# Turning the score maxima of a cross-attention round by transfers through device memory instead of on TensorE

## The chip, the cores and the metric

The kernel runs on one core of a Trainium2 chip. The metric is the device time of one execution in microseconds (us), lower is better; runs of the kernel before gave 2155.49, 2155.64 and 2157.81 us, median 2155.64.

## The reference, cut to what matters

The model is two Perceiver layers over 32 batches of 64 latent rows of width 256. Most of the time goes to the cross-attention of the second layer, in which each batch's 64 latents attend, with 16 heads of 16 channels, to a context of 1601 rows:

```
q = query @ Wq.T + bq;  k = bank @ Wk.T + bk;  v = bank @ Wv.T + bv      # bank: (32, 1601, 256)
scores = einsum('bhqd,bhkd->bhqk', q / sqrt(16), k)
attn = softmax(scores, axis=-1)
ctx = einsum('bhqk,bhkd->bhqd', attn, v)
out = ctx @ Wo.T + bo
```

The softmax needs the maximum of each score row over the 1601 keys, and it is this maximum that the change is about. All other parts (self-attention, routed and shared experts, a recurrent block, a quantised feed-forward) are untouched; they run in the gaps of the loop described next.

## The kernel before

Two batches make one tile of 128 latent rows, so there are 16 *positions*. A position is worked in 13 *units* (`NU`): four *halves* (two batches times two groups of eight heads), each cut into three pieces of 512 keys, and one tail unit for the last 65 keys of all four halves. The main loop runs over the 208 units `g`, and in each iteration it does, in this order:

1. `column_scores(g)`: the scores of unit g with the keys on the partitions. Four bfloat16 matmuls (L770; L767 in the tail unit) first put the negative maxima into PSUM: a 3-row operand `neg`, three bfloat16 parts whose sum is the fp32 value, against ones. Then 16 matmuls (L776) add q·k on top, and ScalarE takes exp of the sum (L782), which gives `pt`.
2. `values(g + 4)`: V of a later unit (L230 `vps`), copied out by VectorE into `vau` (L712).
3. `maxima_rows(h)`, in the iterations where a half has been scanned to its end one iteration earlier: TensorE transposes `mxp` (L751) into a PSUM tile `tpm` of the ring `ps_mm`, and VectorE copies it out as `neg` (L753).
4. `run(g, 0)`: a piece of the other layers' work, laid out by a plan.
5. `row_scores(g + 5)`: the same scores with the latents on the partitions, for the maxima alone: eight matmul passes (L728 `r`) into two PSUM tiles of `ps_sc`, and one VectorE maximum over each (L735, L732 for the tail).
6. `maxima(h)`, when unit g + 5 is the last of a half: VectorE reduces to `ng` (128 x 4, negated, L741) and splits it into three bfloat16 parts in `mxp` (L743 to L746).
7. `weighted(g)`: 64 matmul passes of `pt` against `vau` (L800).
8. `keys(g + 6)`: K of a later unit (L230 `kps`), then `run(g, 1)`.

So a half's maxima are reduced at the end of step 6 of one iteration, turned round in step 3 of the next, and first read by step 1 of the one after that. There are 64 halves; the first is treated before the loop.

The order on TensorE, VectorE, ScalarE and GpSimd is the order of the program text; only the queue of SyncE (SP), which issues the loads and stores, is ordered by a scheduler. The halves' PSUM tiles: `r` and `s` share `ps_sc` (two tiles); `vps`, `kps`, `tpm` and the other layers' tiles share the ring `ps_mm` of three, so a tile waits until the tile three before it has been read out.

Of the kernel before, what the change touches and what calls it, by code (L numbers as in the profile page):

```python
# [9 lines left out]
F32 = mybir.dt.float32  # L10
BF16 = mybir.dt.bfloat16
AF = mybir.ActivationFunctionType
ALU = mybir.AluOpType
AX = mybir.AxisListType

P = 128
# [5 lines left out]
NT = NB * S // P  # L22
# [6 lines left out]
NP = L // PIECE  # L29
TAIL = L - NP * PIECE  # L30
NU = 4 * NP + 1
# [13 lines left out]
def perceiver_kernel(ctx: ExitStack, tc: tile.TileContext, a: dict, out: bass.AP):  # L45
    nc = tc.nc
    PSUM = bass.MemoryType.PSUM

    const = ctx.enter_context(tc.tile_pool(name="const", bufs=1))
    work = ctx.enter_context(tc.tile_pool(name="work", bufs=2))  # L50
# [7 lines left out]
    away = loop.enter_context(tc.tile_pool(name="away", bufs=2, space=bass.MemoryType.DRAM))  # L58
# [5 lines left out]
    def sc_tile(name):  # L64
        return ps_sc.tile([P, 2, 512], F32, tag="sc", name=name)
# [4 lines left out]
    def mm_tile(shape, name, dtype=F32):  # L70
        return ps_mm.tile(shape, dtype, tag="mm", name=name)
# [5 lines left out]
    def work_tile(shape, tag, name, dtype=F32):  # L77
        return work.tile(shape, dtype, tag=tag, name=name, bufs=BUFS.get(tag, 1))
# [25 lines left out]
    def load_rest(ti):  # L104

        t = big.tile([P, 2, 2, TAIL], F32, tag="rest", name=f"rest_{ti}", bufs=2)
        for b in range(2):
# [11 lines left out]
    identb = const.tile([P, P], BF16, name="identb")  # L119
# [3 lines left out]
    ones = const.tile([P, P], F32, name="ones")  # L123
# [5 lines left out]
                            base=0, pattern=[[-16, 8]], channel_multiplier=1)  # L129
    nc.gpsimd.affine_select(out=mask8, in_=mask8, compare_op=ALU.is_ge, fill=0.0,  # L130
                            base=15, pattern=[[16, 8]], channel_multiplier=-1)
# [31 lines left out]


    vau = [const.tile([P, 4, VW], F32, name=f"vau{k}") for k in range(5)]
    mxp = [const.tile([P, 4, 32], BF16, name=f"mxp{k}") for k in range(2)]
    for t in vau:
        nc.gpsimd.memset(t, 0.0)
        nc.gpsimd.memset(t[:, :, 0:VW - 16].rearrange("p k (h d) -> p k h d", d=17)[:, :, :, 16:17], 1.0)
    for t in mxp:  # L170
        nc.vector.memset(t, 0.0)


# [85 lines left out]
    def layer0(ti, csum, k=0, soon=False):  # L259
# [151 lines left out]
        for o, w in ((u_ps, w_s1), (v_ps, w_s3)):  # L411
            for oc in range(2):
# [22 lines left out]
                            pattern=[[1, E], [-1, E]], channel_multiplier=0)  # L435
# [211 lines left out]
    def scanned(g):  # L647

        pos, p = divmod(g, NU)
        return (pos, 4 * pos + (p - 1) // NP, (p - 1) % NP) if p else (pos, None, None)  # L650
# [65 lines left out]
    def row_scores(g):  # L716


        pos, h, k = scanned(g)
        w, qbd = wholes[pos], queries[pos]  # L720
        if h is None:
            w.mx = small.tile([P, 4, 4, NP + 1], F32, tag="mx1", name=f"mx1_{w.ti}", bufs=2)
        ps = [sc_tile(f"r_{g}_{m}") for m in range(2)]
        for q in range(4) if h is None else [h % 4]:
            for i in range(4):
                r = slice(32 * i, 32 * i + 32)
                o = ps[i // 2][:, i % 2, :] if h is not None else ps[i // 2][:, i % 2, q * TAIL:(q + 1) * TAIL]
                nc.tensor.matmul(o, lhsT=qbd[r, q % 2, q // 2].rearrange("p h q -> p (h q)"),  # L728
                                 rhs=w.kt[r, q, :] if h is None else halves[h].kt[k][r, :], start=True, stop=True)
        for m in range(2):  # L730
            if h is None:
                nc.vector.tensor_reduce(w.mx[:, 2 * m:2 * m + 2, :, NP],  # L732
                                        ps[m][:, :, :4 * TAIL].rearrange("p i (q l) -> p i q l", q=4), AX.X, ALU.max)
            else:
                nc.vector.tensor_reduce(w.mx[:, 2 * m:2 * m + 2, h % 4, k], ps[m], AX.X, ALU.max)  # L735

    def maxima(h):

        hf = halves[h]
        ng = small.tile([P, 4], F32, tag="ng", name=f"ng_{hf.name}")  # L740
        nc.vector.tensor_reduce(ng, wholes[hf.pos].mx[:, :, h % 4, :], AX.X, ALU.max, negate=True)  # L741
        m = mxp[h % 2]
        nc.vector.tensor_copy(m[:, :, 0], ng)  # L743
        nc.vector.tensor_tensor(ng, ng, m[:, :, 0], ALU.subtract)
        nc.vector.tensor_copy(m[:, :, 1], ng)
        nc.vector.tensor_tensor(m[:, :, 2], ng, m[:, :, 1], ALU.subtract)  # L746

    def maxima_rows(h):
        hf = halves[h]
        t = mm_tile([P, P], f"tpm_{hf.name}", BF16)  # L750
        nc.tensor.transpose(t, mxp[h % 2].rearrange("p i c -> p (i c)"), identb)  # L751
        hf.neg = work.tile([P, P], BF16, tag="neg", name=f"neg_{hf.name}", bufs=5)
        nc.vector.tensor_copy(hf.neg, t)  # L753

    def column_scores(g):
# [399 lines left out]
    def first_layer(pos, k=0):  # L1155
        x3[pos] = yield from layer0(order[pos], csums[pos], k)
# [10 lines left out]
    def first():  # L1167

        csum = sums_tile(order[0])
        steps = layer0(order[0], csum, 0, True)  # L1170
        next(steps)
        yield
        next(steps)
        yield
        next(steps)
        junk = big.tile([P, L], F32, tag="part", name="junk", bufs=1)
        for b in range(2):
            yield
            summed(order[0], csum, b, 0, ctxs[b][:, 0, :], junk)
            nc.vector.tensor_reduce(csum[:, 1, b:b + 1], ctxs[b][:, 1, :], AX.X, ALU.add)  # L1180
        csums[0] = csum
        yield
        x3[0] = yield from steps
        yield from query(0, x3[0])
# [7 lines left out]
    def early_sums():  # L1192
        for pos in range(1, 4):
            yield from sums(pos, 2)
# [3 lines left out]
    def planned(gen, t0, t1, n, place):  # L1198
        plan.append(Steps(gen, t0 * NU / 16, t1 * NU / 16, n, place))
# [20 lines left out]
    with tc.manual_schedule(engines={ET.PE, ET.DVE, ET.Activation, ET.Pool}):  # L1220
        ahead, beside, summing = Steps(first()), Steps(first_layer(1, 1)), Steps(early_sums())
        early = [lambda g=g: keys(g) for g in range(1, 4)] + [lambda: keys(0)] + [
            lambda g=g: values(g) for g in range(4)] + [lambda g=g: keys(g) for g in range(4, 6)]

        def others():
            if 0 in csums:
                summing.step()
            if 1 in csums:
                beside.step()

        ahead.step()
        late = [late_weights]
        while 0 not in queries:
            if early:
                early.pop(0)()
            ahead.step()
            others()
            if 1 in csums and late:
                late.pop()()
        for f in early + late:  # L1240
            f()
        for g in range(4):
            row_scores(g)
            others()
        maxima(0)
        row_scores(4)
        others()
        maxima_rows(0)
        if beside.gen is not None:
            plan.insert(0, Steps(beside.gen, 0, 3, 30 - beside.done, 2))  # L1250
        planned(biased(), 3, 5, 2, 1)
        if summing.gen is not None:
            plan.insert(0, Steps(summing.gen, 0, 5, 12, 0))
        planned(all_ternary(), 5, 23, 24, 2)

        def run(t, place):
            for s in [s for s in plan if s.t0 <= t]:
                s.run(t, place)
                if t >= s.t1 and t < NU * NT - 1:
                    s.all()  # L1260
                if s.gen is None:
                    plan.remove(s)

        for g in range(NU * NT):
            pos, p = divmod(g, NU)
            if pos + 1 < NT:
                if p == 0:
                    wholes[pos + 1].rest = load_rest(order[pos + 1])
                if p in (2, 9):
                    load_batch(2 * pos + 2 + p // 8)  # L1270
            column_scores(g)
            if g + 4 < NU * NT:
                values(g + 4)
            if p == 1 and pos:
                normalise(pos - 1)
            if g + 4 < NU * NT and scanned(g + 4)[2] == NP - 1:
                maxima_rows(scanned(g + 4)[1])
            run(g, 0)
            if g + 5 < NU * NT:
                row_scores(g + 5)  # L1280
                if scanned(g + 5)[2] == NP - 1:
                    maxima(scanned(g + 5)[1])
            weighted(g)
            if p == NU - 1:
                gathered(pos)
            if g + 6 < NU * NT:
                keys(g + 6)
            if p == 1 and pos:
                x4[pos - 1] = projected(pos - 1)
            run(g, 1)  # L1290
        normalise(NT - 1)
        x4[NT - 1] = projected(NT - 1)
        plan.append(Steps(second_layer(NT - 1)))
        while plan:
            for s in list(plan):
                s.step()
                if s.gen is None:
                    plan.remove(s)
# [46 lines left out]
```

## Time and profile before

| | |
|---|---|
| median of the runs | 2155.64 us |
| the profiled execution | 2154.58 us, of which span 2152.9 us |
| `r` matmuls (L728) | 1536 passes, mean 650 ns |
| row maxima (L735) | 384 of 1219 ns |
| transposes (L751) | 64, median 219 ns; their weight load 100 ns |
| copies of `neg` (L753) | 64 of 213 ns |
| `maxima` (L741, L743 to L746) | 64 each of 169, 176, 190, 177 and 177 ns |
| SP queue | 293 rows in the program; moves 129.52 MB, 17.6% of the 16 engines' time |

The granted TensorE clock is 1.00 over nearly all of the loop (0.974 as a mean over the span). The span has 95% of busy TensorE; the loop itself runs from about 94 us to 2080 us. "Busy" of TensorE is modelled and its matmuls overlap, so the distance between starts says more than the durations.

### The profile page before, as it was taken

The numbers are of one execution on the slowest core, as the hardware profiler recorded it, in microseconds if no ns is written. First come the engines' busy times: TensorE is split into PE (matmuls) and PEld (weight loads), VectorE is DVE, ScalarE is ACT, GpSimd is POOL, SyncE is SP. The second block draws the span as 40 slices with busy tenths as digits, with TensorE's granted clock in tenths as the row PEclk, the third lists the DMA queues.
The fourth block names the chain that finished last, engine by engine and source line by source line (L and its number), as shares of the span: only waits on it lengthen the run. The fifth ranks groups of instructions, "written<-read, shape, count | busy, mean of one in ns | idle before, by whom it ended". The sixth has DMA issues, their size and how long they took to land.

```text
span 2152.9 us, 69473 instructions
## 1 busy us (share of the span) xinstructions
PE 2034.8 (95%) x31691; PEld 1482.9 (69%) x31707; DVE 1302.2 (60%) x2614; ACT 907.1 (42%) x1400; POOL 324.7 (15%) x538
## 2 busy tenths in 40 slices
PE   5799999999999999999999999999999999999964
PEld 4567677777776777777777777767776666676753
DVE  4556756666656665665666656565676656565544
ACT  3334454444535444444444435453433334334332
POOL 2211211111112111112111111111100111000011
PEclk8799999999999999999999999999999999999986
DMA  7233212221212222112221212211111111101000
GB/s 267 84 107 115 95 66 75 68 75 35 74 67 71 73 68 67 45 66 75 68 75 40 91 33 79 75 38 42 45 45 32 47 42 35 54 2 45 2 14 5
DMA packets 52654, 134.77 MB, mean 63 GB/s; under 512 B 12894, under 2 KB 32776, under 8 KB 52360
## 3 DMA queue, kind: packets, MB, share of 16 engines
q1 hardware_dynamic: 51800, 129.52, 17.6%
q8 instruction: 248, 4.06, 0.8%
q10 hardware_dynamic: 560, 0.81, 0.1%
q14 instruction: 46, 0.38, 0.1%
HBM read 124.02 MB, written 6.29 MB: 61 GB/s over the span
## 4 chain that ended last, share of the span: by engine, by line
PE 84%; DVE 9%; ACT 3%; DMA 2%; issue 1%; POOL 1%; SPq 0%; POOLq 0%; DVEq 0%; ACTq 0%
PE vps L230 17%; PE kps L230 16%; PE r L728 10%; PE o L800 9%; PE s L776 8%; PE ff L230 4%; DVE mx L735 3%; PE s L770 3%; PE ffo L951 2%; PE q L230 1%; ACT pt L782 1%; PE wo L230 1%; PE hg L902 1%; PE s L330 1%; PE v L316 1%
## 5 line engine op out<-in xcount | busy, mean ns | idle before, releaser
L735 DVE TENSOR_REDUCE mx<-r 128x2 f32<-128x1024 f32 x384 | 451.9, 1219 | 131.2 <-PE r L728 131.1
L782 ACT ACTIVATE pt<-s 128x1024 f32<-128x1024 f32 (+1 forms) x416 | 403.0, 1020 | 286.0 <-PE s L776 285.8
L695 ACT ACTIVATE kt<-kps,chv 128x512 f32<-128x512 f32 x192 | 131.9, 687 | 636.1 <-PE kps L230 636.1
L230 PE MATMUL kps<-ctxT,w_L_xattn_WkT 128*128 128x512 f32 x768 | 384.5, 624 | 11.9 <-DMA ctxT<-ctxT 11.9
L230 PE MATMUL vps<-w_L_xattn_WvT,ctxT 128*128 128x128 f32 x3072 | 394.5, 282 | 0.0
L230 PEld LDWEIGHTS vps<-w_L_xattn_WvT,ctxT 128*128 128x128 f32 x3072 | 358.5, 192 | 23.7 <-issue 2.8
L712 DVE COPY vau<-vps 128x512 f32<-128x512 f32 (+1 forms) x208 | 143.4, 689 | 370.4 <-PE vps L230 370.4
L800 PEld LDWEIGHTS o<-pt,vau 128*32 128x32 f32 (+1 forms) x13312 | 196.7, 110 | 151.5 <-issue 139.7
L800 PE MATMUL o<-pt,vau 128*32 128x64 f32 (+1 forms) x13312 | 231.2, 221 | 5.3 <-ACT pt L782 5.2
L728 PE MATMUL r<-kt,qbd 32*128 32x512 f32 x1536 | 230.3, 650 | 1.9 <-DVE mx L735 1.1
L230 PEld LDWEIGHTS kps<-ctxT,w_L_xattn_WkT 128*128 128x128 f32 x768 | 132.0, 191 | 124.4 <-issue 107.5
L776 PEld LDWEIGHTS s<-qbd,kt 32*128 32x128 f32 x6144 | 206.2, 187 | 3.1
L776 PE MATMUL s<-qbd,kt 32*128 32x128 f32 x6144 | 207.3, 271 | 0.0
L242 ACT ACTIVATE part<-part 128x1601 f32<-128x1601 f32 x60 | 92.6, 1543 | 16.9 <-DMA part<-ctxT 16.6
L728 PEld LDWEIGHTS r<-kt,qbd 32*128 32x128 f32 x1536 | 65.7, 185 | 40.8 <-issue 18.5
L770 PE MATMUL s<-neg,onesb 3*128 3x512 bf16 x768 | 80.4, 385 | 6.7 <-DVE mx L735 4.5
L770 PEld LDWEIGHTS <-onesb 3*128 3x128 bf16 x768 | 20.9, 91 | 94.2 <-issue 92.5
L230 PE MATMUL ff<-nT,w_fg 128*128 128x128 f32 x384 | 51.7, 287 | 1.0 <-ACT nT L938 1.0
L308 POOL TENSOR_TENSOR kbd<-kT,mask 128x512 f32<-128x512 f32 x32 | 32.7, 1043 | 129.9 <-ACT kT L301 129.9
L230 PEld LDWEIGHTS ff<-nT,w_fg 128*128 128x128 f32 x384 | 47.8, 200 | 1.9 <-ACT nT L938 1.8
L230 PE MATMUL ff<-nT,w_fv 128*128 128x128 f32 x384 | 48.9, 278 | 0.0
L230 PEld LDWEIGHTS ff<-nT,w_fv 128*128 128x128 f32 x384 | 46.5, 196 | 0.0
(329 smaller groups left out, 2435.7 us busy)
## 6 DMA issues: line engine op xcount, KB each, us to landing
ctxT<-ctxT SPq DMA_DIRECT2D x32, 1601.0 KB
part<-ctxT SPq DMA_DIRECT2D x60, 800.5 KB
od<-osb SPq DMA_DIRECT2D x16, 256.0 KB
rest<-ctxT SPq DMA_DIRECT2D x32, 65.0 KB
x<-x SPq DMA_DIRECT2D x16, 128.0 KB
rs<-od SPq DMA_DIRECT2D x32, 64.0 KB
og<-od SPq DMA_DIRECT2D x32, 64.0 KB
out<-x SPq DMA_DIRECT2D x16, 128.0 KB
```

The source lines that it names most:

```text
L230: nc.tensor.matmul(o, lhsT=lhsT(c), rhs=rhs(c), start=(c == 0), stop=(c == 1))
L242: nc.scalar.activation(junk, src, AF.Copy, accum_out=csum[:, c, b:b + 1])
L308: nc.gpsimd.tensor_tensor(kbd[oc], kT[:, oc, :].rearrange("p (b k) -> p b k", b=2).unsqueeze(2).to_broadcast([P, 2, 4, S]), mask4.unsqueez ...
L695: nc.scalar.activation(kt, o, AF.Identity, bias=chv[:, hf.oc, BK2:BK2 + 1])
L712: nc.vector.tensor_copy(v[:kr, :, 0:VW - 16].rearrange("p k (h d) -> p k h d", d=17)[:, :, :, 0:16], o[:kr].rearrange("p k (h d) -> p k h ...
L728: nc.tensor.matmul(o, lhsT=qbd[r, q % 2, q // 2].rearrange("p h q -> p (h q)"), rhs=w.kt[r, q, :] if h is None else halves[h].kt[k][r, :], ...
L735: nc.vector.tensor_reduce(w.mx[:, 2 * m:2 * m + 2, h % 4, k], ps[m], AX.X, ALU.max)
L770: nc.tensor.matmul(o, lhsT=onesb[r, :], rhs=halves[h].neg[r, :].unsqueeze(1).to_broadcast([3, 4, P]), start=True, stop=False)
L776: nc.tensor.matmul(ps[i // 2][:kr, i % 2, j * P:(j + 1) * P], lhsT=w.kt[r, j, :] if h is None else halves[h].kt[k][r, j * P:(j + 1) * P], ...
L782: nc.scalar.activation(pt[:kr].rearrange("p i k c -> p i (k c)"), ps[m][:kr], AF.Exp)
L800: nc.tensor.matmul(w.o[32 * c:32 * c + 32, q, m, :], lhsT=v[:kr, j, 17 * hd:17 * hd + 32], rhs=pts[m][:kr, c // 2, j, c % 2 * S:c % 2 * S ...
L951: nc.tensor.matmul(o, lhsT=m[:, f, :], rhs=w_fo[:, f, :], start=(f == 0), stop=(f == NF - 1))
```

## The change

For every half but the first, `maxima` stops after `ng`. SP writes `ng` (128 x 4) transposed to device memory (4 x 128), then reads each of its four rows back, broadcast to three partitions, into the fp32 tile `mxr` (rows 32i to 32i+2). `maxima_rows` then makes the three bfloat16 parts by rows with four VectorE instructions on 128 x 128 elements and no TensorE; `less` holds 0 or -1 for each partition, so that a first part is subtracted on rows 1 and 2 of each group and a second part on row 2 alone: row 0 ends as the first part, row 1 as the second, row 2 as the third. `maxima_rows` is also moved behind `run(g, 0)` and `row_scores(g + 5)`.

```diff
-    mxp = [const.tile([P, 4, 32], BF16, name=f"mxp{k}") for k in range(2)]
+    mxp = const.tile([P, 4, 32], BF16, name="mxp")
+    mxr = [const.tile([P, P], F32, name=f"mxr{k}") for k in range(2)]
+    less = const.tile([P, 2], F32, name="less")
...
@@ maxima
-        m = mxp[h % 2]
+        if h:
+            od = away.tile([4, P], F32, tag="md", name=f"md_{hf.name}", bufs=3)
+            nc.sync.dma_start(od.rearrange("i q -> q i"), ng)
+            for i in range(4):
+                nc.sync.dma_start(mxr[h % 2][32 * i:32 * i + 3], od[i:i + 1].to_broadcast([3, P]))
+            return
+        m = mxp
...
@@ maxima_rows
+        if h:
+            x = mxr[h % 2]
+            part = work.tile([P, P], BF16, tag="part", name=f"part_{hf.name}", bufs=1)
+            nc.vector.tensor_copy(part, x)
+            nc.vector.scalar_tensor_tensor(x, part, less[:, 0:1], x, ALU.mult, ALU.add)
+            nc.vector.tensor_copy(part, x)
+            nc.vector.scalar_tensor_tensor(hf.neg, part, less[:, 1:2], x, ALU.mult, ALU.add)
+            return
...
@@ main loop
-            if g + 4 < NU * NT and scanned(g + 4)[2] == NP - 1:
-                maxima_rows(scanned(g + 4)[1])
             run(g, 0)
             if g + 5 < NU * NT:
                 row_scores(g + 5)
+            if g + 4 < NU * NT and scanned(g + 4)[2] == NP - 1:
+                maxima_rows(scanned(g + 4)[1])
+            if g + 5 < NU * NT:
                 if scanned(g + 5)[2] == NP - 1:
                     maxima(scanned(g + 5)[1])
             weighted(g)
```

In the built programs TensorE loses 63 transposes with their weight loads, and SP gains 63 writes and 252 reads.

More of the change, by code (lines that the diff above doesn't have):

```diff
@@ L165, in perceiver_kernel @@
     vau = [const.tile([P, 4, VW], F32, name=f"vau{k}") for k in range(5)]
-    mxp = [const.tile([P, 4, 32], BF16, name=f"mxp{k}") for k in range(2)]
+    mxp = const.tile([P, 4, 32], BF16, name="mxp")
+    mxr = [const.tile([P, P], F32, name=f"mxr{k}") for k in range(2)]
+    less = const.tile([P, 2], F32, name="less")
+    for j in range(2):
+        t4 = work_tile([P, 4], "oT", f"less{j}")
+        nc.gpsimd.affine_select(out=t4, in_=ones[:, 0:4], compare_op=ALU.is_equal, fill=0.0,
+                                base=-1 - j, pattern=[[-32, 4]], channel_multiplier=1)
+        nc.vector.tensor_reduce(less[:, j:j + 1], t4, AX.X, ALU.add, negate=True)
+    nc.vector.tensor_tensor(less[:, 0:1], less[:, 0:1], less[:, 1:2], ALU.add)
     for t in vau:
@@ L169, in perceiver_kernel @@
         nc.gpsimd.memset(t[:, :, 0:VW - 16].rearrange("p k (h d) -> p k h d", d=17)[:, :, :, 16:17], 1.0)
-    for t in mxp:
+    for t in [mxp] + mxr:
         nc.vector.memset(t, 0.0)
@@ L749, in maxima_rows @@
         hf = halves[h]
+        hf.neg = work.tile([P, P], BF16, tag="neg", name=f"neg_{hf.name}", bufs=5)
+        if h:
[6 more added lines that the diff above has]
+            return
         t = mm_tile([P, P], f"tpm_{hf.name}", BF16)
-        nc.tensor.transpose(t, mxp[h % 2].rearrange("p i c -> p (i c)"), identb)
-        hf.neg = work.tile([P, P], BF16, tag="neg", name=f"neg_{hf.name}", bufs=5)
+        nc.tensor.transpose(t, mxp.rearrange("p i c -> p (i c)"), identb)
         nc.vector.tensor_copy(hf.neg, t)
```

## The prediction
> **What bounds the kernel now.** I read the page first: engine shares, then the chain that ended last. Then the windows, since a share of the whole span mixes the loop with its ends.
>
> ```profile
> PE 2034.8 (95%) x31691; PEld 1482.9 (69%) x31707; DVE 1302.2 (60%) x2614; ACT 907.1 (42%) x1400; POOL 324.7 (15%) x538
> ...
> PE 84%; DVE 9%; ACT 3%; DMA 2%; issue 1%; POOL 1%; SPq 0%; POOLq 0%; DVEq 0%; ACTq 0%
> ```
>
> ```profile
> 400.00:700.00 300.00, 295.54 (x4855) 216.62 (x4856) 188.55 (x376) 142.08 (x218) 49.76 (x76) 1.00 0.20 67
> ```
>
> TensorE (PE, second number of the window) is busy 295.5 of 300 us in mid-loop, with the clock at 1.00: it is the bound, and there is almost no idle time in which a late input could hide. VectorE (DVE) has 37% free, but its place in the order matters, which only the timeline shows. Here is one place where a half's maxima are turned round (the half whose maxima were reduced at 986.6):
>
> ```profile
> 989.63 0.10 PEld L751 LDWEIGHTS <-mxp 128*128 128x128 bf16 x1
> 989.74 0.22 PE L751 MATMUL tpm<-identb,mxp 128*128 128x128 bf16 x1
> 989.74 1.42 PEld L230 LDWEIGHTS ff<-nT,w_fg 128*128 128x128 f32 x12
> ...
> 990.55 0.21 DVE L753 COPY neg<-tpm 128x128 bf16<-128x128 bf16 x1
> ...
> 993.80 2.36 DVE L735 TENSOR_REDUCE mx<-r 128x2 f32<-128x1024 f32 x2 [0.19 <-PE r L728]
> ...
> 996.64 0.39 PE L770 MATMUL s<-neg,onesb 3*128 3x512 bf16 x4
> ```
>
> See two things. The weight load after the transpose starts 0.11 us after the transpose's own. And the two row maxima end at 993.80 + 2.36 = 996.16, while the first matmul that reads `neg` starts at 996.64, right behind `kps`, with no wait: 0.48 us later. In the kernel before, `neg` has then been ready for nearly 6 us.
>
> **What is removed.** 63 transposes. What is one worth? The row says 219 ns, 13.8 us in all. [...] TensorE overlaps its matmuls, and I take the step instead: in the median place 0.11 us from weight load to next weight load. 63 x 0.11 = **7.0 us**. The 63 copies of `neg` (213 ns) leave VectorE, off the path.
>
> A side gain: `tpm` no longer takes a place in the three-tile ring. In 12 of the 63 places a tile soon behind it waits for the copy of `vps`, the tile three before:
>
> ```profile
> 1022.64 0.27 PEld L382 LDWEIGHTS o<-pT,vbd 128*32 128x32 f32 x16 [0.74 <-DVE vau L712]
> ```
>
> These waits sum to 7.4 us (0.2 to 0.74 each). Without `tpm` the next tile of the ring inherits the wait, after a further 0.2 to 1 us of matmuls, so part of it is gone. Between 0 and 7.4, I take half: **4 us**.
>
> **What is added on VectorE, and moved.** Four dependent instructions behind the maxima of `row_scores(g + 5)`. The nearest rows, one for each form:
>
> ```profile
> L120 DVE CAST identb<-ident x1: 194/194/194, 7.3 to 7.3; 128x128 bf16<-128x128 f32 x1
> ```
>
> ```profile
> L871 DVE SCALAR_TENSOR_TENSOR cT<-ypad,chv,cT 128x128 f32<-128x128 f32 x96 | 34.1, 355 | 3.4
> ```
>
> Two casts at 0.194 and two scalar_tensor_tensor with a per-partition scalar at 0.35. In chains of dependent VectorE instructions (L743 to L746, L871) the next starts 0.035 us after the end of the last; an independent one overlaps its predecessor by 0.08; TensorE starts 0.05 after the VectorE end it waits for. So `neg` can be read 2 x 0.194 + 2 x 0.35 + 3 x 0.035 - 0.08 + 0.05 = **1.16 us** after the row maxima. What goes (L743 to L746 and the copy of `neg`: 4 x 0.18 + 0.21 us) stood earlier on VectorE, where TensorE did not wait for it, so it pays nothing back here.
>
> Against 1.16 stands the distance shown above (0.48). I took it in all 63 places: 23 lie at 0.35 to 0.49, one at 0.85, 39 at 1.32 or more, where `run(g, 1)` puts matmuls between `kps` and the scores. The wait is the sum of 1.16 minus the distance: 22 x 0.67 + 0.8 + 0.3 = **15.9 us**, all on TensorE. Behind the waiting matmul stand the whole unit's scores, exp and `weighted`. Nothing on TensorE was waiting there that could take it up (98.5% busy).
>
> **What is added on the SP queue.** Per half a write of 512 pieces of 4 bytes (the transposed side has no two neighbours together), which must land before four reads are issued. Nearest rows: the write of `osb` and the read that waits for it, and the loads of `rest` (two of 256 pieces of 260 bytes, issued at 272.10 and 272.53).
>
> ```profile
> SPq L819 <- DMA od<-osb: 35.5, 16, 4.0
> ```
>
> ```profile
> 273.00:273.50 0.50, 0.50 (x8) 0.33 (x11) 0.00 (x0) 0.01 (x1) 0.00 (x0) 1.00 0.46 96
> 273.50:274.00 0.50, 0.50 (x19) 0.40 (x18) 0.00 (x0) 0.07 (x1) 0.00 (x0) 1.00 0.58 110
> 274.00:274.50 0.50, 0.50 (x6) 0.31 (x8) 0.00 (x0) 0.50 (x2) 0.00 (x0) 1.00 0.29 60
> 274.50:275.00 0.50, 0.50 (x8) 0.00 (x0) 0.00 (x0) 0.50 (x3) 0.00 (x0) 1.00 0.00 0
> ```
>
> The DMA share (next to last) shows 512 small pieces done in some 1.2 us, beginning 0.6 us after the second issue. So: write 0.8 to its first piece, 1.2 of pieces, 0.35 to the signal; three further issues of 0.5 (as `rs` and `og`); 1.3 for the last read: **5.2 us** from `ng` to the four rows. From `ng` to where VectorE wants them (after the next iteration's row maxima) are 6.6 us or more in 62 places, 3.8 in the last. I set SP's new order against the times at which each load is released in the trace: in no place is SP still held by something ahead when `ng` is ready, though in about ten a load of 0.8 or 1.6 MB was issued shortly before and its packets push the write back by 1.5 to 2.4 us. Two places come out late, which costs **1.3 us**. The loads that now stand behind these transfers move by up to 5 us; each has more than that to spare or is unmoved.
>
> The unknown is the 4-byte write; no row has pieces that small. From below it is the 1.2 us of 260-byte pieces, or less. [...]
>
> The set-up of `less` and `mxr` (two GpSimd and three VectorE instructions, some memsets) lies beside the first loads (TensorE's first result comes at 15.6 us): nothing; uncovered, 1 us.
>
> **The sum**, against the profiled execution's 2154.58: - 7.0 - 4 + 15.9 + 1.3 = +6.2, so 2160.8. The median of the runs is 1.1 above that execution: **2162 us**.
>
> **The rivals.**
> - *The maxima's parts hide after all* (faster). If the four instructions were done in 0.5 us, or TensorE took the delay up in idle time later, only the gains remain: -11 us, **2144.6**. For it: VectorE is 60% busy. Against: the four depend on each other, and TensorE has 1.5% idle.
> - *Gain and wait cancel* (no change; 0.2%, 4.3 us, is about what a measurement of this kernel tells from no change). At 0.85 us for the four, as if the scalar_tensor_tensor took 0.2, the 23 places cost about 8.3 + 1.3 and the ring gives 4: **2154 to 2157**.
> - *The transfers come late* (slower). The write decides: with 3 us of pieces the late places add 5 us, with 4 they add 18 (23 places late), with 5 about 41. It decides from about 3.5 us on; at 4 the time is **2180**. [...]
> - *That the change doesn't do what it says*: no; 63 of 64 transposes are gone from TensorE's list.
>
> **How the numbers follow.** Forecast (late `neg`, transfers in time) 0.5, cancel 0.15, hidden 0.18, late transfers 0.17. The forecast's own range is 2155 to 2169 (gain 7 to 14.4, wait 13 to 19), so a tenth of the whole falls under 0.2% above the median. No change is that tenth and nearly all of the cancel case; faster is the hidden case and a little of the cancel case. Low end 2146 takes in half of the hidden case, high end 2181 all but the slowest writes. Faster 0.19, same 0.24, slower 0.57.
>
> **What would show it.** `neg` (L774's output) ending about 1.1 us after the row maxima in all places and TensorE's L795 matmul waiting for it some 0.65 us in about 23: right. No such wait: hidden. VectorE's first copy waiting for a DMA on `mxr`: the write is slower than 1.2 us. Fewer L712 waits: the ring's 4 us. What would make it wrong: a price of the 4-byte write, or scalar_tensor_tensor with a bfloat16 operand at another speed than L871.

## The result, and the profile after

The changed kernel takes 2421.42 us (median of 4 runs, 2415.42 to 2426.29), beside 2155.56 us for the kernel before on the same chip: a ratio of 1.1227, 95% interval 1.1214 to 1.124. The direction was the forecast's; the size, 266 us in place of 6, is far outside its range. The profiled execution has a span of 2419.6 us.

The page of the changed kernel, engine shares (busy us, share of the span, instructions) and the chain that ended last:

```profile
PE 2137.8 (88%) x31628; PEld 1564.1 (65%) x31644; DVE 1321.2 (55%) x2555; ACT 907.6 (38%) x1400; POOL 322.4 (13%) x540
...
PE 52%; DMA 25%; DVE 15%; issue 4%; SPq 2%; ACT 2%; POOL 1%; DVEq 0%; POOLq 0%; ACTq 0%
DMA md<-ng 19%; PE vps L240 13%; PE kps L240 7%; PE s L801 6%; DVE mx L745 6%; PE r L738 6%; DMA mxr<-md 5%; PE o L825 4%; PE ff L240 2%; PE s L795 2%; SPq L757 2%; DVE rs L852 1%; PE q L240 1%; DVE mxr L772 1%; DVE neg L774 1%
```

Two things are to be read here. The chain has moved: DMA had 2% of it and has 25%, and 19% is one transfer, `md<-ng`, the write of 2 KB in 512 pieces. And TensorE is not only idle longer but busy longer: 2137.8 us for 63 transposes fewer, against 2034.8. Span less busy time gives 281.8 us of idle TensorE against 118.1, so the 266.7 us between the two spans are 163.7 us of idleness and 103.0 us of slower work. Most of the slower work is the clock: its mean is 0.929 against 0.974. Counted over the time in which TensorE is busy (half clock while it stands still costs nothing), the trace has 130 us lost against 34, or 97 more. Since the missing transposes take off about 63 x 0.22 = 14, some 20 us of slower work remain that are not the clock; they were not taken apart.

The groups (busy us, mean ns of one | idle before, and what ended it), and SP's waits (us in total, times, longest):

```profile
L771 DVE CAST part<-mxr 128x128 bf16<-128x128 f32 x63 | 14.3, 227 | 194.3 <-DMA mxr<-md 194.1
L772 DVE SCALAR_TENSOR_TENSOR mxr<-part,less,mxr 128x128 f32<-128x128 bf16 x63 | 22.1, 351 | 2.4 <-DVE part L771 0.2
L792 PE MATMUL s<-neg,onesb 3*65 3x128 bf16 x256 | 12.7, 247 | 38.6 <-DVE neg L774 38.6
L795 PE MATMUL s<-neg,onesb 3*128 3x512 bf16 x768 | 84.7, 405 | 110.8 <-DVE neg L774 103.9 <-DVE mx L745 4.5 <-DVE neg L778 2.1
L825 PE MATMUL o<-pt,vau 128*32 128x64 f32 (+1 forms) x13312 | 246.6, 223 | 26.9 <-issue 21.6 <-ACT pt L807 4.5
```

```profile
SPq L757 <- DMA md<-ng: 499.2, 59, 10.2
```

TensorE waits 103.9 + 38.6 = 142.5 us for `neg`, and stops 21.6 us longer in `weighted` (26.9 at L825 against 5.3 at L800 before), together 164.1, as much as the whole of the added idleness (some of the waits for `neg` were foreseen: 15.9). The first sum leads back through VectorE's 194 us wait for the rows to SP, which waits 499 us in 59 places for the write before it may issue the reads. One place, from the timeline (start, us; in brackets the idle time before and who ended it):

```profile
1119.02 0.17 DVE L751 TENSOR_REDUCE ng<-mx 128x4 f32<-128x16 f32 x1
...
1119.22 0.38 SPq L755 DMA_DIRECT2D md<-ng  x1
...
1127.61 1.22 SPq L757 DMA_DIRECT2D mxr<-md  x4
...
1131.23 0.23 DVE L771 CAST part<-mxr 128x128 bf16<-128x128 f32 x1 [2.79 <-DMA mxr<-md]
1131.50 0.35 DVE L772 SCALAR_TENSOR_TENSOR mxr<-part,less,mxr 128x128 f32<-128x128 bf16 x1
1131.88 0.23 DVE L773 CAST part<-mxr 128x128 bf16<-128x128 f32 x1
1132.14 0.35 DVE L774 SCALAR_TENSOR_TENSOR neg<-part,less,mxr 128x128 bf16<-128x128 bf16 x1
...
1132.55 0.39 PE L795 MATMUL s<-neg,onesb 3*128 3x512 bf16 x4 [2.46 <-DVE neg L774]
```

From the write's issue to the first read's issue pass 8.39 us. Over all 63 places this distance, which the experiments below are measured by, has a median of 8.68 us (7.67 to 10.63); the forecast had 2.4. From `ng` to the rows it is 12.0 us here and 12.1 in the median, not 5.2. What the write does in this time can be seen by the DMA share of the windows behind it (next to last number):

```profile
1120.00:1121.00 1.00, 1.00 (x16) 0.88 (x12) 0.90 (x2) 0.69 (x1) 0.00 (x0) 1.00 0.25 2
1121.00:1122.00 1.00, 1.00 (x11) 1.00 (x10) 0.00 (x0) 1.00 (x2) 0.93 (x1) 1.00 0.00 0
1122.00:1123.00 1.00, 1.00 (x11) 1.00 (x10) 0.66 (x1) 0.25 (x1) 0.98 (x1) 1.00 0.00 0
1123.00:1124.00 1.00, 1.00 (x11) 1.00 (x11) 0.03 (x1) 0.32 (x1) 0.00 (x0) 1.00 0.00 0
1124.00:1125.00 1.00, 1.00 (x13) 0.88 (x12) 0.56 (x1) 0.17 (x1) 0.00 (x0) 1.00 0.00 0
```

The 512 packets are recorded between 1120.1 and 1120.5, 7 to 9 ns each. Then the windows show no packets, and still the write is not done for another 7 us. SP is not what is late: the semaphore for which it waits is raised in steps (26 of the 63 writes have 16 of them in the trace, none has more), and of this write 13 steps are in the trace, from 5.34 to 8.36 us after the issue. (In the 56 places with most of the steps in the trace, the first comes at 6.4 us and the last at 8.7 in the median; for the write in row order below it is 1.2 and 1.9.) Here the packet records do not show when a write is complete: the last packet starts 1.25 us after the issue, the last step comes at 8.7 (medians).

The lost clock, in the windows around another late place, where TensorE had stood still for 4.37 us up to 1100.02 (granted clock: third number from the end):

```profile
1098.00:1100.00 2.00, 0.00 (x0) 0.00 (x0) 1.19 (x5) 0.00 (x0) 0.00 (x0) 0.84 0.00 0
1100.00:1102.00 2.00, 1.97 (x36) 1.89 (x36) 1.63 (x3) 0.00 (x0) 0.95 (x2) 0.50 0.34 131
1102.00:1104.00 2.00, 2.00 (x16) 1.78 (x13) 0.00 (x0) 1.55 (x2) 1.68 (x1) 0.50 0.05 18
1104.00:1106.00 2.00, 2.00 (x12) 1.77 (x11) 0.00 (x0) 2.00 (x4) 0.79 (x2) 0.50 0.23 75
1106.00:1108.00 2.00, 2.00 (x71) 1.24 (x72) 1.45 (x2) 0.30 (x2) 0.00 (x0) 0.96 0.41 103
```

After the stall the clock is 0.50 for 6 us: by these windows the stall of 4.4 us costs some 3 us more once it is over.

### The profile page after: what moved, and what is told of

It reads as the page before. It is cut to its first block, busy times and chain, and to the rows that moved or that the text cites. A ratio compares the mean times of both kernels' runs of the same rounds, so it can differ in the third digit from the quotient of the medians.

```text
span 2419.6 us, 69772 instructions
## 1 busy us (share of the span) xinstructions
PE 2137.8 (88%) x31628; PEld 1564.1 (65%) x31644; DVE 1321.2 (55%) x2555; ACT 907.6 (38%) x1400; POOL 322.4 (13%) x540
## 4 chain that ended last, share of the span: by engine, by line
PE 52%; DMA 25%; DVE 15%; issue 4%; SPq 2%; ACT 2%; POOL 1%; DVEq 0%; POOLq 0%; ACTq 0%
DMA md<-ng 19%; PE vps L240 13%; PE kps L240 7%; PE s L801 6%; DVE mx L745 6%; PE r L738 6%; DMA mxr<-md 5%; PE o L825 4%; PE ff L240 2%; PE s L795 2%; SPq L757 2%; DVE rs L852 1%; PE q L240 1%; DVE mxr L772 1%; DVE neg L774 1%
## 5 line engine op out<-in xcount | busy, mean ns | idle before, releaser
L807 ACT ACTIVATE pt<-s 128x1024 f32<-128x1024 f32 (+1 forms) x416 | 403.1, 1021 | 472.1 <-PE s L801 471.9
L240 PE MATMUL vps<-w_L_xattn_WvT,ctxT 128*128 128x128 f32 x3072 | 437.3, 301 | 0.0
L240 PEld LDWEIGHTS vps<-w_L_xattn_WvT,ctxT 128*128 128x128 f32 x3072 | 400.4, 211 | 27.3 <-issue 9.3
L240 PE MATMUL kps<-ctxT,w_L_xattn_WkT 128*128 128x512 f32 x768 | 393.9, 637 | 11.5 <-DMA ctxT<-ctxT 11.5
L825 PEld LDWEIGHTS o<-pt,vau 128*32 128x32 f32 (+1 forms) x13312 | 204.9, 111 | 179.9 <-issue 168.8
L825 PE MATMUL o<-pt,vau 128*32 128x64 f32 (+1 forms) x13312 | 246.6, 223 | 26.9 <-issue 21.6
L801 PEld LDWEIGHTS s<-qbd,kt 32*128 32x128 f32 x6144 | 224.8, 202 | 4.2
L801 PE MATMUL s<-qbd,kt 32*128 32x128 f32 x6144 | 226.7, 288 | 0.0
L795 PE MATMUL s<-neg,onesb 3*128 3x512 bf16 x768 | 84.7, 405 | 110.8 <-DVE neg L774 103.9
L771 DVE CAST part<-mxr 128x128 bf16<-128x128 f32 x63 | 14.3, 227 | 194.3 <-DMA mxr<-md 194.1
```

What stands on the lines that cost most here:

```text
L240: nc.tensor.matmul(o, lhsT=lhsT(c), rhs=rhs(c), start=(c == 0), stop=(c == 1))
L795: nc.tensor.matmul(o, lhsT=onesb[r, :], rhs=halves[h].neg[r, :].unsqueeze(1).to_broadcast([3, 4, P]), start=True, stop=False)
L801: nc.tensor.matmul(ps[i // 2][:kr, i % 2, j * P:(j + 1) * P], lhsT=w.kt[r, j, :] if h is None else halves[h].kt[k][r, j * P:(j + 1) * P], ...
L807: nc.scalar.activation(pt[:kr].rearrange("p i k c -> p i (k c)"), ps[m][:kr], AF.Exp)
L825: nc.tensor.matmul(w.o[32 * c:32 * c + 32, q, m, :], lhsT=v[:kr, j, 17 * hd:17 * hd + 32], rhs=pts[m][:kr, c // 2, j, c % 2 * S:c % 2 * S ...
```

## The experiments

All ratios are to the kernel before on the same chip, with 95% intervals; "first read" is the median distance just defined.

**Which part of the change costs?** Four edits of the changed kernel (the third of the kernel before).

The write in row order, 128 pieces of 16 bytes:

```diff
-            nc.sync.dma_start(od.rearrange("i q -> q i"), ng)
+            nc.sync.dma_start(od.rearrange("i q -> (i q)").rearrange("(q i) -> q i", i=4), ng)
```

> The write of the maxima goes to device memory in the order of its rows (128 pieces of 16 bytes instead of 512 of 4); the reads and everything else stay, so the rows read back are not the maxima of those rows. Theory A (the 4-byte write lands late, about 8.4 us after its issue, and the bf16 parts come late for TensorE): the first read is issued some 2.0 to 2.5 us after the write, the rows are there 6 us after the reduction, and the time falls to 2150 to 2172 us. Theory B (the new place of maxima_rows and its four VectorE instructions cost the time): stays within 20 us of 2421. Theory C (the many small packets hold up other transfers and instruction loads): falls too; e3 tells A from C.

The transfers taken out, the four VectorE instructions left at their new place on a constant tile:

```diff
-            nc.sync.dma_start(od.rearrange("i q -> q i"), ng)
-            for i in range(4):
-                nc.sync.dma_start(mxr[h % 2][32 * i:32 * i + 3], od[i:i + 1].to_broadcast([3, P]))
```

> No write and no reads: the four VectorE instructions work at the new place on a constant tile, so the maxima themselves are left out. Theory A: 2155 to 2168 us (my sum without the transfers: -7.0 - 4 + 15.9 = +5), with TensorE waiting some 0.65 us for neg in about 23 places. Theory B: about 2400. Theory C: as A.

The kernel before with the same transfers beside its own path, read by nobody:

```diff
+        if h:
+            od = away.tile([4, P], F32, tag="md", name=f"md_{hf.name}", bufs=3)
+            nc.sync.dma_start(od.rearrange("i q -> q i"), ng)
+            for i in range(4):
+                nc.sync.dma_start(mxr[h % 2][32 * i:32 * i + 3], od[i:i + 1].to_broadcast([3, P]))
```

> The kernel before, with the transposes on TensorE, and besides the 63 writes and 252 reads of the change, whose result nobody waits for. Theory A: 2150 to 2165 us (nothing is late). Theory C: at least a third of the loss is there, 2240 us or more. Theory B says nothing here.

The changed kernel with `row_scores` and `keys` one unit further ahead, so that the rows have a whole iteration more:

```diff
-            if g + 5 < NU * NT:
-                row_scores(g + 5)
+            if g + 6 < NU * NT:
+                row_scores(g + 6)
...
-            if g + 6 < NU * NT:
-                keys(g + 6)
+            if g + 7 < NU * NT:
+                keys(g + 7)
```

> The changed kernel with row_scores and keys one unit further ahead (one more buffer for K), so that the transfers have an iteration, some 9 to 10 us, more. Theory A: 16 us or more stand against the 12.3 that the transfers take, so they are in time and only the four instructions are left: 2155 to 2175 us. Theory B and C: still near 2400.

| | us | ratio | first read |
|---|---|---|---|
| write in row order | 2166.14 | 1.0051 (1.0031 to 1.007) | 2.02 us |
| no transfers | 2164.27 | 1.0039 (1.0025 to 1.0054) | |
| unread transfers | 2215.42 | 1.0286 (1.0261 to 1.031) | 8.54 us |
| one unit earlier | 2250.58 | 1.0438 (1.0399 to 1.0477) | |

With the pieces in row order the time is where the forecast had it, and so is the first read (one unit earlier, still 94 us above the kernel before, comes back below). Only the write was changed, so it is the transposed write that costs. But it costs in two ways: even when nobody waits for it, it takes 59 us, between what the two theories had expected (24.5 us of idle TensorE and 34.3 us of slower work, by the page of this run). The timeline of the unread transfers shows one place:

```profile
563.62 0.54 PE L807 MATMUL o<-pt,vau 128*32 128x64 f32 x23
566.96 0.81 PE L807 MATMUL o<-pt,vau 128*32 128x64 f32 x12 [2.80 <-issue]
568.51 0.80 PE L807 MATMUL o<-pt,vau 128*32 128x64 f32 x15 [0.74 <-issue]
```

```profile
558.23 0.37 SPq L745 DMA_DIRECT2D md<-ng  x1
560.22 0.35 SPq L96 DMA_DIRECT2D part<-ctxT  x1
568.74 0.27 SPq L747 DMA_DIRECT2D mxr<-md  x1
```

While the write of 558.23 is under way (it lets the read go at 568.74), TensorE stops in the middle of the 64 passes of `weighted`, twice (2.80 and 0.74 us), and "issue" says that it waited for nothing that the profile shows. The eight longest pauses of this kind at L807 (1.03 to 2.80 us) all begin 5.9 to 9.1 us behind such a write. In the same run the 248 packets of the queue that loads instructions take 1.34 us in the mean and up to 4.16, against 1.07 and 1.66 before. That TensorE runs out of instructions because their loading is held up by the write is a guess, and the trace does not bear it out everywhere: the last such packet before the longest pause (at 562.97) took 1.29 us, no longer than some do in the kernel before, and was over when most of the pause was still to come. By what way the write stops TensorE stays open.

**Is it the place, the pieces' number, or the direction?** The kernel without transfers, with `maxima_rows` at its old place:

```diff
+            if g + 4 < NU * NT and scanned(g + 4)[2] == NP - 1:
+                maxima_rows(scanned(g + 4)[1])
             run(g, 0)
```

> As e2 (no write, no reads, four VectorE instructions on a constant tile), but maxima_rows stands where it stood before, ahead of run(g, 0). If the wait of TensorE for the four instructions is what e2 pays (my 15.9 us) and 63 transposes with their place in the ring are worth 11 us: 2141 to 2150 us, 12 to 20 under e2. If e2's 8 us over the kernel before came from elsewhere: within 5 us of e2.

A write in row order, and the turning done by the reads, 384 pieces of 4 bytes each:

```diff
+            od = away.tile([P, 4], F32, tag="md", name=f"md_{hf.name}", bufs=3)
+            nc.sync.dma_start(od, ng)
...
+                nc.sync.dma_start(mxr[h % 2][32 * i:32 * i + 3], od[:, i:i + 1].rearrange("q i -> i q").to_broadcast([3, P]))
```

> The maxima are written as they stand (128 pieces of 16 bytes, as in e1) and turned round by the four reads, which now gather 128 pieces of 4 bytes for each of three partitions. Theory A1 (a small piece is dear where device memory is written): the first read is issued 2 us after the write, TensorE's instruction loads are not held up, and the time lies between e1 and the change, 2170 to 2300 us, as the gathering reads take some 3 to 6 us more than plain ones. Theory A2 (512 or more pieces are dear on either side): 2420 us or more.

Half the pieces, two rows in place of four, each read twice:

```diff
+            nc.sync.dma_start(od[0:2].rearrange("i q -> q i"), ng[:, 0:2])
...
+                nc.sync.dma_start(mxr[h % 2][32 * i:32 * i + 3], od[i % 2:i % 2 + 1].to_broadcast([3, P]))
```

> Two of the four columns are written (256 pieces of 4 bytes) and read twice, so half of the maxima is left out; the rest as in the change. A price for each piece: from the write's issue to the first read about 5 us instead of 8.7, the rows some 3.5 us earlier, 2230 to 2310 us. A fixed price for a write with pieces so small: still 8 us or more, about 2400.

The same 512 pieces of 4 bytes, each in a cell of 64 bytes of its own:

```diff
+    apart = [away.tile([4, P, 16], F32, tag=f"md{k}", name=f"md{k}", bufs=1) for k in range(3)]
...
+            od = apart[h % 3]
+            nc.sync.dma_start(od[:, :, 0].rearrange("i q -> q i"), ng)
...
+                nc.sync.dma_start(mxr[h % 2][32 * i:32 * i + 3], od[i:i + 1, 0:8, :].rearrange("o a b -> o (a b)").to_broadcast([3, P]))
```

> The 512 pieces of 4 bytes go each into a 64-byte cell of its own instead of side by side; the reads take as many contiguous bytes from the same buffer (one maximum in sixteen elements, the others a constant), and three more loads at the start fill the buffers (some us). If pieces that share a stretch of memory wait for one another, the first read follows the write after 2 to 4 us and the time falls under 2250. If each small piece costs by itself: 8 us or more and 2400 or more, as in the change.

| | us | ratio | first read |
|---|---|---|---|
| no transfers, old place | 2152.89 | 0.9987 (0.9978 to 0.9996) | |
| turned by the reads | 2323.41 | 1.0775 (1.0746 to 1.0803) | 1.95 us |
| half the pieces | 2451.57 | 1.1368 (1.1347 to 1.1389) | 8.57 us |
| pieces apart | 2165.57 | 1.0044 (1.003 to 1.0059) | 2.10 us |

Half the pieces take as long as all of them (8.57 us and 8.68): the price is not so much per piece. The same number of pieces, apart from each other, takes 2.1 us: nor is it the 4 bytes or the rearranged pattern by itself. What was changed is how densely the 4-byte pieces lie in device memory (2 KB for all of them, or 32 KB). In the timeline of the kernel with the pieces apart:

```profile
1050.57 0.37 SPq L760 DMA_DIRECT2D md<-ng  x1
1052.67 1.20 SPq L762 DMA_DIRECT2D mxr<-md  x4
```

and in its waits, for `neg`, as the forecast had them:

```profile
PE s L800 <- DVE neg L779: 15.4, 24, 0.8
```

Half the pieces (two runs) is slower still than the change: in its trace the four reads take 3.9 us from the first issue to the last signal (median), in place of 3.2, so the rows come at 12.5 us, not 12.1. Why these reads take longer stays open. Turning by the reads fails in another way, and lies above the 2300 us expected: the write is quick, but the four reads of 384 pieces take 4.5 us to issue (median) in place of 1.2, and 8.4 us to the last signal in place of 2.4 with the plain reads behind the same quick write. VectorE then waits 122.5 us for the rows. One place, in which a load of 800 KB issued at 1115.82 stands just ahead and the write takes 3.9 us instead of the usual 1.95:

```profile
1117.05 0.34 SPq L755 DMA_DIRECT2D md<-ng  x1
1120.97 4.30 SPq L757 DMA_DIRECT2D mxr<-md  x4
```

**How near is too near?** The cells made smaller (8 words as shown for 32 bytes; 4 and 2 words for 16 and 8), and the unread transfers repeated with cells of 64 bytes:

```diff
-    apart = [away.tile([4, P, 16], F32, tag=f"md{k}", name=f"md{k}", bufs=1) for k in range(3)]
+    apart = [away.tile([4, P, 8], F32, tag=f"md{k}", name=f"md{k}", bufs=1) for k in range(3)]
```

> As the kernel with each 4-byte piece in a cell of 64 bytes, but with cells of 32 bytes, so that two pieces share each 64 bytes of device memory. Part left out as there: what is read back is a constant. Theory A (writes into one 64-byte stretch are done one behind another, each further piece costs (8.6 - 2.1) / 15 = 0.43 us): first read issued about 2.5 us after the write, still in time, ratio 1.004 to 1.006. Rival B (any sharing of a 64-byte stretch costs the whole price): 8 us or more, ratio above 1.08. Rival C (it is the touching of neighbours or the small extent of memory that counts): 2.1 us, ratio 1.0044 as with 64 bytes.

> Cells of 16 bytes: four pieces in each 64 bytes. What is read back is a constant. Theory A: 2.1 + 3 x 0.43 = 3.4 us from the write's issue to the first read's, some places late, ratio 1.005 to 1.01. Rival B: 8 us or more, above 1.08. Rival C: 2.1 us, 1.0044.

> Cells of 8 bytes: eight pieces in each 64 bytes, none touching another. What is read back is a constant. Theory A: 2.1 + 7 x 0.43 = 5.1 us to the first read, many places late, ratio 1.015 to 1.04. Rival B: 8 us or more, above 1.08. Rival C: 2.1 us, 1.0044.

> The kernel before with the transfers added that nobody reads, as in the earlier run, but the pieces written into cells of 64 bytes. If the sharing of stretches is what held up TensorE there too: ratio 0.999 to 1.004, the mean of the instruction-loading packets back at 1.07 to 1.10 us, TensorE's waits without a releaser at the weight loads of weighted back from 169 to about 140 us. If it is the mere number of packets (512 writes and 12 reads a half): 1.02 to 1.03 as with the pieces side by side.

| cell | pieces to 64 bytes | first read | added by each further piece | ratio |
|---|---|---|---|---|
| 64 bytes | 1 | 2.10 us | | 1.0044 (1.003 to 1.0059) |
| 32 bytes | 2 | 2.32 us | 0.22 us | 1.004 (1.0026 to 1.0055) |
| 16 bytes | 4 | 2.87 us | 0.26 us | 1.0065 (1.005 to 1.008) |
| 8 bytes | 8 | 4.26 us | 0.31 us | 1.0066 (1.0049 to 1.0084) |
| 4 bytes (the change) | 16 | 8.68 us | 0.44 us | 1.1227 (1.1214 to 1.124) |

The time grows with how densely the pieces lie, by (first read - 2.10) / (pieces - 1) for each further one. Neither "all or nothing" (rival B) nor "only touching pieces" (rival C) fits. That pieces near each other are written one behind another (theory A) fits the growth, but not at the fixed price of 0.43 us, and the ratio of 1.015 to 1.04 that it expected for 8 bytes was too high; such a queue is argued from the table, not seen. How long the stretch is within which pieces wait, the table can't tell, since a longer one would grow in the same way; 64 bytes is only its unit. Four pieces of 16 bytes to 64 bytes (the write in row order, 2.02 us) paid nothing, so the count to a stretch is not the whole rule; there the pieces are larger, fewer, and neighbours follow one another in the pattern, and which of these matters was not tried.

With cells of 8 bytes the reads are 2 us later than with 64, and the time is only 5 us longer: the slack of 6.6 us that the forecast had found still covers nearly all of it. The unread transfers with the pieces apart take 2156.33 us, ratio 0.9999 (0.9989 to 1.0008). So the disturbance goes with the density too, not with the number of packets; instruction packets take 1.11 us and the pauses are gone. The `weighted` group without transfers (before), with unread dense ones, and with unread ones apart:

```profile
L800 PE MATMUL o<-pt,vau 128*32 128x64 f32 (+1 forms) x13312 | 231.2, 221 | 5.3 <-ACT pt L782 5.2
```

```profile
L807 PE MATMUL o<-pt,vau 128*32 128x64 f32 (+1 forms) x13312 | 245.4, 223 | 28.8 <-issue 23.8 <-ACT pt L789 4.7
```

```profile
L812 PE MATMUL o<-pt,vau 128*32 128x64 f32 (+1 forms) x13312 | 231.7, 221 | 5.3 <-ACT pt L794 5.2
```

**The change whole, with only the layout altered.** In the runs with cells the rows read back were a constant. Here the cells of 32 bytes are read back whole and VectorE takes the first word of each; the maxima are real:

```diff
-    mxr = [const.tile([P, P], F32, name=f"mxr{k}") for k in range(2)]
+    mxr = [const.tile([P, P, 8], F32, name=f"mxr{k}") for k in range(1)]
...
+            od = apart[h % 3]
+            nc.sync.dma_start(od[:, :, 0].rearrange("i q -> q i"), ng)
...
+                nc.sync.dma_start(mxr[0][32 * i:32 * i + 3].rearrange("p q b -> p (q b)"), od[i:i + 1].rearrange("o q b -> o (q b)").to_broadcast([3, 8 * P]))
...
+            x = mxr[0][:, :, 0]
```

> The change itself, complete, with one edit: the pieces are written into cells of 32 bytes, the cells are read back whole (4096 bytes to each of 12 partitions, one buffer), and VectorE takes the first word of each cell. If the sharing of 64-byte stretches is the whole of what the forecast missed: 2.3 us to the first read, ratio 1.003 to 1.007, that is 2162 to 2171 us. If the reading or something else of the change adds to it: above 1.01.

The same with `maxima_rows` at its old place, and then also with everything one unit earlier (there with cells of 16 bytes):

> As e15_cells_all_read, but maxima_rows stays at its place before run(g, 0) and row_scores(g + 5). The rows are wanted some 3 us earlier, but neg a whole iteration before TensorE reads it. If the rows are in time (about 5.5 us after ng): ratio 0.998 to 1.001, as without transfers at the old place (0.9987). If VectorE waits for them there and holds up the copy of V behind it: 1.002 to 1.02.

> As e17_cells_old_place, with row_scores and keys one unit earlier, and cells of 16 bytes. The rows have an iteration more, so nobody can wait for them. If being one unit earlier costs nothing in itself and the 95 us of the earlier run were all the disturbance by the write: 0.998 to 1.001. If being earlier costs by itself what is left of the 95 us beside the unread transfers (61 us): 1.01 to 1.015.

| | us | ratio |
|---|---|---|
| new place | 2179.62 | 1.0113 (1.0098 to 1.0128) |
| old place | 2192.18 | 1.0172 (1.0146 to 1.0199) |
| old place, one unit earlier | 2161.86 | 1.0027 (1.0016 to 1.0038) |

The layout is worth 2421.4 - 2179.6 = 242 of the 266 us. The first of the three lies 8.6 us above the 2171 that it was to reach if the layout were all. A part of this is its own: reading every eighth word makes the VectorE chain longer (452 and 270 ns for the 352 and 222 with the pieces apart), and TensorE waits 22.7 + 2.3 us for `neg` where it waited 15.4 + 0.6.

```profile
L777 DVE SCALAR_TENSOR_TENSOR mxr<-part,less,mxr 128x128 f32<-128x128 bf16 x63 | 28.5, 452 | 2.2
...
L776 DVE CAST part<-mxr 128x128 bf16<-128x128 f32 x63 | 17.0, 270 | 2.5 <-DMA mxr<-md 2.4
```

At the old place VectorE reaches the rows before they are there, and what stands behind its wait, the row maxima among it, comes later (TensorE waits 18.6 us for the row maxima at L800, against 6.6 without transfers; the rest of the loss was not taken apart):

```profile
L776 DVE CAST part<-mxr 128x128 bf16<-128x128 f32 x63 | 19.8, 314 | 54.8 <-DMA mxr<-md 54.6
```

One unit earlier that wait is gone and 2162 us remain. So being earlier costs little by itself (2161.9 beside the 2152.9 without transfers at the old place, cells of 16 bytes and all), and it was not this that cost the earlier run with the dense pieces its 94 us. Nor was it lateness: its TensorE waited 15.4 us for `neg` as in the quick kernels, but 37.6 us with "issue" in `weighted`. The disturbance as seen with the unread transfers (59) and the new place (11) make 70 of the 94. The pauses are longer here than with the unread transfers (37.6 us against 23.8), so the disturbance is larger too; the other 24 us were not taken apart further. None of the complete versions beats the kernel before, and the run without any transfer at the old place says why: all that taking the transposes off TensorE brings there is 0.13%, some 3 us.

## Why the prediction was wrong

- **What bounds the kernel, and where the slack is**: right. TensorE at 98.5% in mid-loop, `neg` needed at once after `kps`, 6.6 us for the transfers. The kernels with row order or cells of 32 or 64 bytes land at 2164 to 2166 us, the forecast being 2162. That the sum comes so near is in part luck: its gain was too large by about 8 us and its price for the move by about 4, and these cancel in part (both below).
- **The gain (-7.0 and -4)**: too large. Without transfers and at the old place, where 12 to 20 us less than at the new place were expected, the kernel gains 2.8 us by the ratio (0.9 to 4.7 by the interval) in place of 11. In that run the waits of TensorE's weight loads for the copy of `vps` fall from 15.4 to 9.7 us over all tiles, near the 4 us assumed for the ring; the 7.0 us for the transposes' steps are not to be seen beside it.
- **The wait for `neg` (+15.9)**: right. It is 15.4 us in the runs with the pieces apart, in row order and without transfers; L771 to L774 took 227, 351, 226 and 351 ns for the 194 and 350 assumed. Moving costs 2164.3 - 2152.9 = 11.4 us of time.
- **The price of the write: the step that failed.** "Write 0.8 to its first piece, 1.2 of pieces, 0.35 to the signal" is 2.4 us; it took 8.7. The first two terms hold or are too long (the packets start 0.9 to 1.25 us behind the issue in the median place); what failed is the third, the 0.35 us from the last packet to the last signal, which is over 7 us. The row chosen, the loads of `rest`, shows pieces on their way *into* the core, each into memory of its own; nothing in it is like 16 pieces that go to the same 64 bytes of device memory. With pieces apart the 2.4 us would have been right (2.10). The reads behind it were nearly right: 3.2 us from the first issue to the last signal, for the 2.8 assumed.
- **The rival "the transfers come late"** was the right mechanism and had 0.17, but its scale (18 us at 4 us of pieces, 41 at 5) counted only the lateness itself. The waits for `neg` came to 142.5 us, some 127 more than with a quick write. Two costs had no term: the half clock around the longer stalls (97 us more lost), and the disturbance of TensorE by the write even where nobody waits for it (59 us when measured alone).

## What to carry to other kernels

Here a write of 4-byte pieces that lie densely in device memory could not be priced by its bytes, its packets or a row of loads. Time such a write from its issue to the first instruction that waits for it; if it is slow, try the pieces further apart (8.7 us became 2.1), or larger ones in row order (2.0, though here that leaves the turning undone). Where TensorE is at 98%, price a late input by more than its lateness: here the half clock took 97 us more than before, beside 164 us of added idleness. And first ask what the whole removal can bring, by a kernel that leaves out the new path: here it was 3 us, which no transfer could have been worth.

## What the runs showed of the hardware

- In the changed kernel's trace 512 pieces of 4 bytes, packed into 2 KB of device memory, take 8.7 us from the write's issue to the first read that waits for it, although the last of their packets starts 1.25 us after the issue (medians); by the same measure they take 2.1 us in the run with cells of 64 bytes; 256 packed into 1 KB take 8.6 in the run with half the pieces; 128 pieces of 16 bytes packed into 2 KB take 2.0 in the run in row order.
- In the run with such writes that nobody reads, packets that load instructions take longer (mean 1.34 us against 1.07 before, and 1.11 with the pieces apart), and behind the writes TensorE pauses for up to 2.8 us with nothing to wait for that the profile shows.
- In the loop of the changed kernel's trace all of the 20 stalls of TensorE of 3.5 us or more have half the clock behind them, and so have 11 of the 14 between 2.0 and 3.5 us. In this trace it comes in stretches of 3.4 or 6.8 us (once 10.2), which can begin within the stall; behind the 20 it lasts 5 us in the median.
